# Causal attention on TensorE: scores by blocks of 32 queries instead of 64, values in four rounds, tokens in natural order

## The chip, the core and the metric

The kernel runs on one core of a Trainium2 chip, as one program. The time is device microseconds of one execution; each version is executed several times and the median counts. The engines have their own instruction streams: TensorE (PE in the profile; PEld is its weight load), VectorE (DVE), ScalarE (ACT), GpSimd (POOL) and SyncE (SP), on whose queue nearly all DMAs are issued one after another. TensorE multiplies from SBUF into the accumulation memory PSUM; a matmul has a weight tile, which is loaded first, and streams columns past it. Every value here is fp32, and an fp32 matmul leaves two matmul records in the trace.

## The reference

The input x has 64 sequences of 128 tokens and 512 features. There are 16 heads of width 64 that all share one key and one value per token, and one null key and value ahead of the first token.

```python
xn = layernorm(x, g_in)
q = (xn @ Wq).reshape(b, n, H, DH).transpose(0, 2, 1, 3) * scale      # 64 x 16 x 128 x 64
k, v = xn @ Wkv split in two                                           # 64 x 128 x 64 each
k, v = null key and value (from cond) put ahead of the tokens          # 129 keys
sim = einsum('bhid,bjd->bhij', q, k) + bias                            # bias 16 x 128 x 129
sim = where(causal_mask or masked key, -max, sim)
attn = softmax(sim)
out = einsum('bhij,bjd->bhid', attn, v).reshape(b, n, 1024) @ Wo
return x + layernorm(out, g_out)
```

The causal mask lets query i see the null key and the tokens 0 to i. Beside it every sequence has its own mask of valid keys.

## The kernel before, in words

**Stages.** The order of all work on all engines is written out by hand: a function such as `turn` calls helpers, each of which issues the instructions of one step, and each engine takes its instructions in that order. The sequences go in groups of four (GB) and in 32 pairs (PAIRS). One period of the steady state is `turn(d)` and `body(d)`. `turn(d)` (L1024 to L1050) runs the scores of the two sequences a = 2d and b = 2d + 1 and the values of the pair before. `body(d)` (from L1311) runs the projections: queries of the next group by Strassen-like products, keys and values (`kv_pair`, L363), the layernorm of the tokens, and the products with Wo of the pair before. Below a sequence is called a batch, as in the code. The first and last pairs have orders of their own: a start that is written out (L1559 to L1678) and `turn_end`, `body_end` and `body_last`.

**Scores.** The queries of two heads lie above each other on the partitions: rows 0 to 63 one head (r = 0), rows 64 to 127 the other (r = 1). The key tile kT holds the keys twice, on both halves; the upper copy is made by a DMA (L396). A score matmul (L718) uses a 64 by 64 quarter of the array: 64 rows of features and 64 columns of weights, which are 64 queries of one head. So four matmuls, for (r, u) in 2 x 2, run at a time. The queries of a sequence are cut into two halves (hf): half 0, the tokens 0 to 63, gets the first 64 keys (NL); half 1 gets all 128. For each half there are four such groups (f) and four matmuls in each. On the partitions of the result lie 64 queries of head group u = 0 and 64 of u = 1; on the free axis eight heads (R8). A row of S is ROW = 1 + 64 + 128 + 1 = 194 elements: the null key and the keys of half 0, the keys of half 1 and the null key again.

**Softmax.** `bias_add` (L683, GpSimd) fills S with bias plus mask. `scores_add` (L733, L735, VectorE) adds the scores from PSUM. `scores_max` (L740) takes the maximum, `exps` (L749, ScalarE) exponentiates a row (queries on the partitions) of one head and half, with its sum, `rinv` (L767) inverts the sums, `scale` (L771, GpSimd) multiplies. `mask_neg` (L670, ScalarE) turns the byte mask of a group, loaded by `load_mask` (L137), into large negative numbers.

**Values.** `blocks_T` (L787, VectorE) transposes S in blocks of 32 by 32 into the tile sb, so that 32 keys of one block lie on each quarter of the partitions. A values matmul (L849) has 32 rows (the keys of block j) by 64 columns (the values, vr); quarter s of the rows holds the queries of block s. Eight places, (s, r) in 4 x 2, run at a time. In each place four matmuls follow one another, the first with 256 columns and three with 128. `WIDE` merges two of the 128s into one 256 for s = 3 in some turns. The order of tokens within a sequence is changed so that these rounds come out: `PLACE = 0, 1, 3, 2` swaps the third and the fourth block of 32 tokens. For this the copies out of PSUM that write the transposed tokens xT (`norm_T`, L313 and L315) and the keys kT (`kv_pair_out`, L380 to L396) are made in three pieces. `values_out` (L868, L870, ScalarE) copies the result with the null value added to oT.

**The start.** `load_bias` (L193 to L203) loads the bias of the heads in the layout of S with six DMAs for each u (L198 and L200), called from `load_second` (L177). It stands on SP's queue ahead of the key copies (L396) that `kv_pair_out` issues, of `load_mask(0)` and of the copies of the values by way of DRAM (`values_T`, vd L406 and vr L411). `causal` (L212, GpSimd) writes the causal mask into the bias, three instructions for each u; `null_shift` (L225, L229, VectorE) subtracts the null key's bias. On ScalarE `mask_neg(0)` stands ahead of the copies of qT for `q_batches((6,))` (L459) and of `norm_T(6)`; the first scores, `scores(0, 0)`, come on TensorE behind `norm_T(7)`. The very first matmuls of the program are `keep_busy` (L1556), products of the identity that nobody reads.

Of the kernel before, what the change touches and what calls it, by code (L numbers as in the profile page):

```python
# [17 lines left out]
def kernel(  # L18
# [63 lines left out]
    P = 128  # L82
# [11 lines left out]
    NL = DH  # L94
    ROW = 1 + NL + N + 1
    LK, UK = slice(1, 1 + NL), slice(1 + NL, 1 + NL + N)
    assert NQ == GB and NQ == KC
    PLACE = 0, 1, 3, 2
# [48 lines left out]
    nbp = const.tile([P, R8], FP, name="nbp")  # L147
    nv2 = const.tile([P, 1], FP, name="nv2")
    nbh = const.tile([P, H], FP, name="nbh")
    biasp = const.tile([P, R8, ROW], FP, name="biasp")  # L150
# [42 lines left out]
    def load_bias(u):  # L193
        rows = slice(u * DH, (u + 1) * DH)
        bias_r = attn_bias.rearrange("(u f r) i j -> u r i f j", u=2, r=2)[u]
        for r in range(2):
            rf = slice(r * NF, (r + 1) * NF)
            nc.sync.dma_start(out=biasp[rows, rf, LK], in_=bias_r[r, 0:DH, :, 0:NL])  # L198
            for i, at in enumerate((N - Q, N - 2 * Q)):
                nc.sync.dma_start(  # L200
                    out=biasp[u * DH + i * Q : u * DH + (i + 1) * Q, rf, UK],
                    in_=bias_r[r, at : at + Q],
                )  # L203

    def causal(u):

        for rows, keys, base in (
            (slice(u * DH, (u + 1) * DH), LK, 0),
            (slice(u * DH, u * DH + Q), UK, N - Q),
            (slice(u * DH + Q, (u + 1) * DH), UK, N - 2 * Q),  # L210
        ):
            nc.gpsimd.affine_select(  # L212
                biasp[rows, :, keys],
                biasp[rows, :, keys],
                pattern=[[0, R8], [-1, keys.stop - keys.start]],
                compare_op=ALU.is_ge,
                fill=NEG,
                base=base,
                channel_multiplier=1,
            )  # L220

    def null_shift(u):

        rows = slice(u * DH, (u + 1) * DH)
        nc.vector.tensor_copy(  # L225
            nbp[rows].rearrange("p (r f) -> p r f", r=2),
            nbh[rows, u * R8 : (u + 1) * R8].rearrange("p (f r) -> p r f", r=2),
        )
        nc.vector.tensor_tensor(  # L229
            biasp[rows, :, 1 : ROW - 1],  # L230
            biasp[rows, :, 1 : ROW - 1],
            nbp[rows].unsqueeze(2).broadcast_to([DH, R8, NL + N]),
            ALU.subtract,
        )
# [11 lines left out]
    nc.gpsimd.memset(biasp[0:DH], 0.0)  # L246
    nc.gpsimd.memset(biasp[DH:, :, 0 : ROW : ROW - 1], 0.0)
# [7 lines left out]
    nc.gpsimd.memset(mneg[:, :, 0 : ROW : ROW - 1], 0.0)  # L255

# [49 lines left out]
    def norm_T(m):  # L306
        g, t = divmod(m, GB)
        if t == 0:
            xT[g] = gp.tile([P, GB, KC, N], FP, tag="xT", name=f"xT_{g}")
        xh = xs.pop(m)  # L310
        pt = ps_w.tile([P, KC, P], FP, tag="w", name=f"pxT_{m}")
        for kc in range(KC):
            nc.tensor.transpose(pt[:, kc, :], xh[:, kc * P : (kc + 1) * P], ident)  # L313
        for at, to, n in ((0, 0, 2), (3, 2, 1), (2, 3, 1)):
            nc.scalar.copy(  # L315
                xT[g][:, t, :, to * Q : (to + n) * Q], pt[:, :, at * Q : (at + n) * Q]
            )
# [3 lines left out]
    def tokens_T(m):  # L321

        g, t = divmod(m, GB)
        if t == 0:
            xbs[g] = hp.tile([P, NQ, KC, NQ, Q], FP, tag="xb", name=f"xb_{g}", bufs=1)
        nc.vector.transpose(
            xbs[g][:, :, :, PLACE[t], :].rearrange("p j c q -> p c j q"),
# [22 lines left out]
    kT = hp.tile([P, NQ, GB, Q], FP, tag="kT", name="kT", bufs=1)  # L350
# [24 lines left out]
    def kv_pair_out(m, pkv):  # L375
# [11 lines left out]
        src = pkv[K_ROWS].rearrange("p (t i q) -> p t i q", t=2, i=NQ)  # L387
        out = kT[K_ROWS, :, two].rearrange("p i t q -> p t i q")
        for at, to, n in ((0, 0, 2), (3, 2, 1), (2, 3, 1)):
            nc.scalar.activation(  # L390
                out[:, :, to : to + n],
                src[:, :, at : at + n],
                AF.Identity,
                bias=nkv[K_ROWS],
            )
        nc.sync.dma_start(out=kT[V_ROWS, :, two], in_=kT[K_ROWS, :, two])  # L396
# [31 lines left out]
    def q_tiles(g, fs, tags):  # L428
        units = [(f, h) for f in fs for h in range(2)]
        for (f, h), tag in zip(units, tags):  # L430
            qT[g, f, h] = gp.tile(
                [P, GB // 2, 2, 2, DH], FP, tag=tag, name=f"qT_{g}_{f}_{h}", bufs=1
# [25 lines left out]
    def q_copy(pq, c, h):  # L458
        nc.scalar.copy(  # L459
            q_part(0, c, h), pq.rearrange("p t (h i) -> p t h i", h=2)  # L460
        )
# [67 lines left out]
    def q_out(g, c, h, tag, name=None):  # L529
        o = q_part(g, c, h)  # L530
        p = prod[tag].rearrange("p (t h i) -> p t h i", t=2, h=2)
        if name is None:
            nc.scalar.copy(o, p)
        else:
            k = kept.pop(name).rearrange("p (t h i) -> p t h i", t=2, h=2)
# [54 lines left out]
    def inner_out(g, h, f, t, at, name=None):  # L590

        o = q_part(g, 2 * h + f, 0)[:, t]
        p = inner[g, h][:, at].rearrange("p (h i) -> p h i", h=2)
        k = o
        if name is not None:
            k = kept[name].rearrange("p (t h i) -> p t h i", t=2, h=2)[:, t]
# [59 lines left out]
    def last_out(g, h, f, t, at, first=False):  # L656

        o = q_part(g, HC + 2 * h + f, 0)[:, t]
        p = last_area(g, h, at).rearrange("p (h i) -> p h i", h=2)
        k = o  # L660
        if first:
            k = base[f].rearrange("p (t h i) -> p t h i", t=2, h=2)[:, t]
# [4 lines left out]
    def mask_neg(g):  # L667
        m8 = m8s.pop(g).rearrange("p (t j) -> p t j", t=GB)
        for keys, m in ((LK, m8[:, :, 0:NL]), (UK, m8)):
            nc.scalar.activation(  # L670
                mneg[:, :, keys], m, AF.Identity, bias=neg, scale=-NEG
# [4 lines left out]
    def bias_add(b, parts=(slice(0, ROW),)):  # L676
        g, t = divmod(b, GB)
        if b < B - 1:
            S[b] = sp.tile([P, R8, ROW], FP, tag="s", name=f"s_{b}", bufs=3)
        else:  # L680
            S[b] = hp.tile([P, R8, ROW], FP, tag="xb", name=f"s_{b}", bufs=1)
        for keys in parts:
# [5 lines left out]
                .broadcast_to([P, R8, keys.stop - keys.start]),  # L688
# [3 lines left out]
    KEYS = LK, UK  # L692
    WITH_NULL = slice(0, 1 + NL), slice(1 + NL, ROW)

    def rooms(b, hf, tiles):

        nk = N if hf == 1 else NL
        return [
            pool.tile([P, NF, nk], FP, tag=tag, name=f"sc_{b}_{hf}_{tag}")
# [3 lines left out]
    def scores(b, hf, tiles=None):  # L703
        g, t = divmod(b, GB)
        nk = N if hf == 1 else NL
        if tiles is None:
            whole = ps_s.tile([P, 2, NF * nk], FP, tag="s", name=f"ps_{b}_{hf}")
            whole = whole.rearrange("p r (f j) -> p r f j", f=NF)
# [5 lines left out]
        for f in range(NF):  # L714
            for r in range(2):
                rows = slice(r * DH, (r + 1) * DH)
                for u in range(2):
                    nc.tensor.matmul(  # L718
                        home[r][u * DH : (u + 1) * DH, f, :],
                        qT[g, f, t // 2][rows, t % 2, hf, u],  # L720
                        kT[rows, 0 : nk // Q, t, :],
                        start=True,
                        stop=True,
                    )
# [12 lines left out]
    def scores_max(b, hf):  # L737
        if hf == 0:
            nmax[b] = small.tile([P, 2, R8], FP, tag="nmax", name=f"nmax_{b}")
        nc.vector.tensor_reduce(  # L740
            nmax[b][:, hf], S[b][:, :, WITH_NULL[hf]], AX.X, ALU.max, negate=True
        )

    def exps(b, hf, lo=0, hi=R8):
        if hf == 0 and lo == 0:
            rsum[b] = small.tile([P, 2, R8], FP, tag="rsum", name=f"rsum_{b}")
        for k in range(lo, hi):
            row = S[b][:, k, WITH_NULL[hf]]
# [20 lines left out]
    def scale(b, hf, lo=0, hi=R8):  # L769
        sv = S[b][:, lo:hi, KEYS[hf]]  # L770
        nc.gpsimd.tensor_tensor(  # L771
            sv,
            sv,
            rinvs[b, hf][:, lo:hi].unsqueeze(2).broadcast_to([P, hi - lo, sv.shape[2]]),
            ALU.mult,
        )
# [6 lines left out]
    def blocks_T(b, lo=0, hi=R8):  # L783

        if lo == 0:
            sbs[b] = hp.tile([P, 6, R8, Q], FP, tag="sb", name=f"sb_{b}")
        nc.vector.transpose(  # L787
# [936 lines left out]
```

## Time and profile before

| | us |
|---|---|
| median of three runs | 1023.52 |
| lowest and highest of them | 1023.01, 1023.75 |
| span of the profiled execution | 1021.2 |
| TensorE busy in it | 1012.8 (99%) |
| VectorE busy | 845.8 (83%) |
| GpSimd busy | 769.2 (75%) |
| ScalarE busy | 673.1 (66%) |

The span runs from the first to the last instruction that the profile shows; the runs' times hold a little more around it, 2.3 us by the median. A row of the groups has line, engine, operation, tiles and shapes, the count, then the busy time, the mean of one in ns and the idle time ahead of it. The chain and the timeline have start and length in us, engine, what, and how many records stand in a row; "[1.35 <-POOL neg L245]" means idle before, and what ended it. Overlapping records of TensorE make a group's mean longer than what one adds to the time: four or eight small matmuls run side by side.

### The profile page before, as it was taken

To read this page: it belongs to the slowest core of one execution; us is meant where nothing else is said; L and a number is where in the kernel's file an instruction comes from. 1 tells how busy PE (TensorE), PEld (TensorE's weight loads), DVE (VectorE), ACT (ScalarE), POOL (GpSimd) and SP (SyncE) were. 2 spreads that over 40 slices of the span, in tenths; PEclk is the share of its full clock that TensorE was granted. 3 is DMA by queue.
4 is the path that set the end of the run, shared out by engine and by line. 5 is a ranking of instruction groups with operands and counts; after the bars stand their busy time and mean duration, and the time that the engine had idled before them with its cause. 6 is when DMAs were issued, how large, how long until landed. Compare 5 with 4: busy or idle time off the path is not lost.

```text
span 1021.2 us, 31459 instructions
## 1 busy us (share of the span) xinstructions
PE 1012.8 (99%) x12333; PEld 899.6 (88%) x12333; DVE 845.8 (83%) x1958; ACT 673.1 (66%) x2753; POOL 769.2 (75%) x633
## 2 busy tenths in 40 slices
PE   9999999999999999999999999999999999999997
PEld 8888888888888888888888888888888888888886
DVE  6777888888888888888888888888898888977787
ACT  5766677656677665686656776566775657865583
POOL 4997768677686877859678696776868768686686
PEclk9999999999999999999999999999999999999999
DMA  7415143151531415225152341514315152140221
GB/s 219 139 30 151 67 122 112 36 154 63 144 98 69 123 56 152 88 74 140 36 152 85 109 120 32 164 63 138 102 50 134 64 152 89 71 111 24 69 85 62
DMA packets 73835, 100.86 MB, mean 99 GB/s; under 512 B 32212, under 2 KB 36056, under 8 KB 71896
## 3 DMA queue, kind: packets, MB, share of 16 engines
q1 hardware_dynamic: 73392, 98.47, 32.5%
q8 instruction: 96, 1.57, 0.6%
q14 instruction: 51, 0.42, 0.1%
q10 hardware_dynamic: 296, 0.40, 0.1%
HBM read 63.19 MB, written 33.55 MB: 95 GB/s over the span
## 4 chain that ended last, share of the span: by engine, by line
PE 96%; POOL 1%; DVE 1%; ACT 1%; issue 0%; DMA 0%; POOLq 0%; DVEq 0%; ACTq 0%
PE pyX L936 20%; PE pa L515 16%; PE pyY L936 10%; PE pc L515 10%; PE po L849 8%; PE pkv L363 6%; PE pyw L936 5%; PE pl L581 4%; PE pm L647 4%; PE ps L718 3%; PE pq L450 3%; PE sc_X L718 2%; PE sc_Y L718 2%; PE sc_a L718 1%; PE py_s L936 1%; ACT s L749 1%
## 5 line engine op out<-in xcount | busy, mean ns | idle before, releaser
L749 ACT ACTIVATE s<-s,nmax 128x65 f32<-128x65 f32 (+1 forms) x1024 | 372.2, 369 | 61.7 <-DVE nmax L740 61.7
L771 POOL TENSOR_TENSOR s<-s,rinv 128x512 f32<-128x512 f32 (+1 forms) x132 | 190.6, 1446 | 133.1 <-DVE rinv L767 133.1
L683 POOL TENSOR_TENSOR s<-biasp,mneg 128x1552 f32<-128x1552 f32 (+1 forms) x65 | 206.2, 3176 | 50.9 <-DVE s L733 26.9
L749 ACT ACTIVATION_READ_ACCUMULATOR s<-s,nmax 128x1 f32 x1024 | 197.1, 192 | 0.0
L787 DVE STREAM_TRANSPOSE sb<-s 128x1536 f32<-128x1536 f32 (+1 forms) x68 | 113.6, 1674 | 11.4 <-POOL s L771 11.4
L740 DVE TENSOR_REDUCE nmax<-s 128x8 f32<-128x1032 f32 (+1 forms) x128 | 121.8, 952 | 0.1
L964 ACT COPY y<-pyX 128x256 f32<-128x256 f32 x29 | 10.8, 372 | 167.5 <-PE pyX L936 129.7
L936 PE MATMUL pyX<-wT,oT 128*128 128x256 f32 x464 | 109.7, 379 | 0.0
L936 PE MATMUL pyX<-wo,oT 128*128 128x256 f32 x464 | 109.7, 379 | 0.0
L936 PEld LDWEIGHTS pyX<-wo,oT 128*128 128x128 f32 x464 | 86.0, 190 | 10.5
L936 PEld LDWEIGHTS pyX<-wT,oT 128*128 128x128 f32 x464 | 84.0, 190 | 9.2
L916 POOL TENSOR_TENSOR oT<-oT 128x512 f32<-128x512 f32 x64 | 80.6, 1277 | 3.9 <-PE pyw L936 1.6
L849 PE MATMUL po<-sb,vr 32*64 32x128 f32 (+1 forms) x3904 | 82.9, 308 | 0.2 <-DVE sb L787 0.2
L527 ACT COPY ku<-pa 128x256 f32<-128x256 f32 x118 | 43.4, 367 | 59.8 <-issue 30.8
L849 PEld LDWEIGHTS po<-sb,vr 32*64 32x64 f32 x3904 | 71.7, 130 | 9.4 <-issue 5.6
L536 DVE TENSOR_TENSOR qT<-pc,ku 128x256 f32<-128x256 f32 x118 | 48.2, 408 | 32.2 <-PE pc L515 19.7
L868 ACT ACTIVATE oT<-po,nv 128x512 f32<-128x512 f32 (+1 forms) x127 | 73.5, 655 | 0.4 <-PE po L849 0.2
L515 PE MATMUL pa<-xS,wq 128*128 128x256 f32 x264 | 67.8, 379 | 0.0
L597 DVE TENSOR_TENSOR qT<-pl,kp 128x128 f32<-128x128 f32 x112 | 32.1, 286 | 42.8 <-PE pl L581 41.9
L281 POOL TENSOR_TENSOR rstd<-rstd,nhalf 128x1 f32<-128x1 f32 x64 | 35.2, 557 | 42.0 <-DVE rstd L280 38.9
L363 PE MATMUL pkv<-xT,wkv 128*128 128x256 f32 x256 | 63.3, 391 | 0.0
L515 PE MATMUL pa<-xT,wq 128*128 128x256 f32 x236 | 60.6, 379 | 0.0
(207 smaller groups left out, 2588.9 us busy)
## 6 DMA issues: line engine op xcount, KB each, us to landing
res<-in_x_dram SPq DMA_DIRECT2D x64, 256.0 KB
out_dram<-y SPq DMA_DIRECT2D x63, 256.0 KB
x<-in_x_dram SPq DMA_DIRECT2D x62, 256.0 KB
xd<-xb SPq DMA_DIRECT2D x14, 1024.0 KB
xT<-xd SPq DMA_DIRECT2D x56, 256.0 KB
vr<-vd SPq DMA_DIRECT2D x64, 128.0 KB
kT<-kT SPq DMA_DIRECT2D x32, 64.0 KB
vd<-vb SPq DMA_DIRECT2D x32, 64.0 KB
```

The lines of the kernel that those rows point to most:

```text
L363: nc.tensor.matmul(pkv, wkv[:, kc, :], xT[g][:, t : t + 2, kc, :], start=(kc == 0), stop=(kc == KC - 1),)
L515: nc.tensor.matmul(prod[tag], w[:, kc, f * P : (f + 1) * P], t[:, :, kc, :], start=(start and kc == 0), stop=(kc == HK - 1), skip_group_ch ...
L683: nc.gpsimd.tensor_tensor(S[b][:, :, keys], biasp[:, :, keys], mneg[:, t, keys] .unsqueeze(1) .broadcast_to([P, R8, keys.stop - keys.start ...
L718: nc.tensor.matmul(home[r][u * DH : (u + 1) * DH, f, :], qT[g, f, t // 2][rows, t % 2, hf, u], kT[rows, 0 : nk // Q, t, :], start=True, st ...
L740: nc.vector.tensor_reduce(nmax[b][:, hf], S[b][:, :, WITH_NULL[hf]], AX.X, ALU.max, negate=True)
L749: nc.scalar.activation(row, row, AF.Exp, bias=nmax[b][:, hf, k : k + 1], accum_out=rsum[b][:, hf, k : k + 1],)
L771: nc.gpsimd.tensor_tensor(sv, sv, rinvs[b, hf][:, lo:hi].unsqueeze(2).broadcast_to([P, hi - lo, sv.shape[2]]), ALU.mult,)
L787: nc.vector.transpose(sbs[b][:, :, lo:hi].rearrange("p j e q -> p e j q"), S[b][:, lo:hi, 1 : ROW - 1].rearrange("p e (j k) -> p e j k", k=Q),
L849: nc.tensor.matmul(po[s][rows, to : to + n], vr[g][quad, t, PLACE[j], :], sb[quad, slots, r * NF : (r + 1) * NF, :], start=(turn == 0), st ...
L868: nc.scalar.activation(to, src, AF.Identity, bias=nv2)
L916: eng.tensor_tensor(o, a, b, op)
L936: nc.tensor.matmul(prod[key], h[:, c, :], w[:, c, :], start=(start and c == 0), stop=(c == HC - 1), skip_group_check=not start,)
```

## The change

Queries are taken in blocks of 32 (i = 0 to 3) instead of 64, and block i gets its own (i + 1) x 32 keys. A weight tile of a score matmul is still 64 columns wide: 32 queries of two heads. A batch has, as before, 64 score matmuls: for each i four groups of four, with 32, 64, 96 and 128 columns where half of them had 64 and half 128. On the partitions of S lie four quarters of 32 queries, each with heads of its own; the free axis has four heads (NE) and ROW = 324 elements, with the keys of the four blocks and a null key at both ends of each half.

- `load_bias`: 16 DMAs for each u instead of six, each for 32 partitions and two heads. `causal`: eight instructions for each u instead of three. `null_shift`: four instead of two.
- `mask_neg`: four instructions for each group instead of two. `scores_max` and `scale`: two for each half, one for each block, instead of one. `exps`: 16 for each batch as before, of 33, 65, 97 and 129 elements instead of 65 and 129. `blocks_T`: three pieces for each batch instead of one.
- `values`: four rounds j = 0 to 3. In round j all eight places run block j of the keys for all later queries, with 256, 192, 128 and 64 columns. `WIDE` is gone. The four quarters are now head groups and not query blocks. `values_out` copies in the order 0, 2, 1, 3.
- Tokens keep their natural order: `PLACE` is gone, and `norm_T` and `kv_pair_out` copy in one piece instead of three.
- At the ends, `turn_end`, `body_end` and `body_last` take over the new pieces; the order of the steps is otherwise as it was, in `turn` and in the start too.

```diff
-    NL = DH
-    ROW = 1 + NL + N + 1
-    PLACE = 0, 1, 3, 2
+    NE = H // NQ
+    NF2 = NF // 2
+    KEYS_OF = tuple((i + 1) * Q for i in range(NQ))
+    ROW = NQ + sum(KEYS_OF)
+    LOW = 2 + sum(KEYS_OF[:2])
+    K_AT = 1, 1 + Q, LOW + 1, LOW + 1 + KEYS_OF[2]
+    BLOCK = tuple(slice(K_AT[i], K_AT[i] + KEYS_OF[i]) for i in range(NQ))
+    KEYS = slice(1, LOW - 1), slice(LOW + 1, ROW - 1)
...
     def load_bias(u):
+        bias_r = attn_bias.rearrange("(v u f r) i j -> u v r i f j", v=2, u=2, r=2)[u]
+        for i in (3, 2, 1, 0):
+            for v in range(2):
+                quad = slice((2 * u + v) * Q, (2 * u + v + 1) * Q)
+                for r in range(2):
+                    nc.sync.dma_start(
+                        out=biasp[quad, r * NF2 : (r + 1) * NF2, BLOCK[i]],
+                        in_=bias_r[v, r, i * Q : (i + 1) * Q, :, 0 : KEYS_OF[i]],
+                    )
...
-        for at, to, n in ((0, 0, 2), (3, 2, 1), (2, 3, 1)):
-            nc.scalar.copy(
-                xT[g][:, t, :, to * Q : (to + n) * Q], pt[:, :, at * Q : (at + n) * Q]
-            )
+        nc.scalar.copy(xT[g][:, t], pt)
...
-        for f in range(NF):
-            for r in range(2):
-                rows = slice(r * DH, (r + 1) * DH)
-                for u in range(2):
-                    nc.tensor.matmul(
-                        home[r][u * DH : (u + 1) * DH, f, :],
-                        qT[g, f, t // 2][rows, t % 2, hf, u],
-                        kT[rows, 0 : nk // Q, t, :],
-                        start=True,
-                        stop=True,
-                    )
+        for i in BLOCKS[hf]:
+            keys = slice(BLOCK[i].start - first, BLOCK[i].stop - first)
+            for f in range(NF2):
+                for r in range(2):
+                    rows = slice(r * DH, (r + 1) * DH)
+                    for u in range(2):
+                        nc.tensor.matmul(
+                            home[r][u * DH : (u + 1) * DH, f, keys],
+                            qT[g, u * NF2 + f, t // 2][rows, t % 2, i],
+                            kT[rows, t, 0 : KEYS_OF[i]],
+                            start=True,
+                            stop=True,
+                        )
...
-    def values(b, wide=()):
+    def values(b):
...
+        for j in range(NQ):
+            slots = slice(j * (1 + SLOT), j + SLOT * SLOT + 1, SLOT)
             for s in range(NQ):
                 quad = slice(s * Q, (s + 1) * Q)
                 for r in range(2):
                     nc.tensor.matmul(
-                        po[s][rows, to : to + n],
-                        vr[g][quad, t, PLACE[j], :],
-                        sb[quad, slots, r * NF : (r + 1) * NF, :],
-                        start=(turn == 0),
+                        pos[b][s][r * DH : (r + 1) * DH, :, j * Q :].rearrange(
+                            "p f (i q) -> p f i q", q=Q
+                        ),
+                        vr[g][quad, t, j, :],
+                        sb[quad, slots, r * NF2 : (r + 1) * NF2, :].rearrange(
+                            "p i f q -> p f i q"
+                        ),
+                        start=(j == 0),
                         stop=True,
...
-        values(p, WIDE if 4 < d < PAIRS - 1 else ())
-        values(p + 1, WIDE if 4 < d < PAIRS - 1 and (d % 2 or d % 10 == 4) else ())
+        values(p)
+        values(p + 1)
```

More of the change, by code (lines that the diff above doesn't have):

```diff
@@ L216, in causal @@
[L216 to L219, printed above, removed]
-            )
[L222 to L227, printed above, removed]
-        )
[L229 to L234, printed above, removed]
+                nbp[rows].unsqueeze(2).broadcast_to([DH, NE, keys.stop - keys.start]),
@@ L386, in kv_pair_out @@
         )
[L387 to L396, printed above, removed]
+        nc.scalar.activation(
+            kT[K_ROWS, two],
+            pkv[K_ROWS].rearrange("p (t n) -> p t n", t=2),
+            AF.Identity,
+            bias=nkv[K_ROWS],
+        )
+        nc.sync.dma_start(out=kT[V_ROWS, two], in_=kT[K_ROWS, two])
     def values_T(g):
@@ L668, in mask_neg @@
         m8 = m8s.pop(g).rearrange("p (t j) -> p t j", t=GB)
-        for keys, m in ((LK, m8[:, :, 0:NL]), (UK, m8)):
+        for keys, n in zip(BLOCK, KEYS_OF):
             nc.scalar.activation(
-                mneg[:, :, keys], m, AF.Identity, bias=neg, scale=-NEG
+                mneg[:, :, keys], m8[:, :, 0:n], AF.Identity, bias=neg, scale=-NEG
             )
```

224 lines of the change are left out of this document (119 added, 105 removed).

## The prediction

> **What bounds the kernel now.** I read the busy times and the chain of waits on the page first, then the chain in order of time for two turns in the middle.
>
> ```profile
> PE 1012.8 (99%) x12333; PEld 899.6 (88%) x12333; DVE 845.8 (83%) x1958; ACT 673.1 (66%) x2753; POOL 769.2 (75%) x633
> ...
> PE 96%; POOL 1%; DVE 1%; ACT 1%; issue 0%; DMA 0%; POOLq 0%; DVEq 0%; ACTq 0%
> ```
>
> TensorE is busy for 99% of the span and 96% of the chain is its matmuls. So a microsecond is won only where TensorE has less to do, and lost where it is made to wait. In the chain below the columns are start, length, what, and the number of records; every fp32 matmul leaves two records.
>
> ```profile
> 511.09 0.67 PE pl L581 x6
> ...
> 527.80 0.20 PE sc_Y L718 x2
> ...
> 528.02 0.04 PE sc_Y L718 x2
> ...
> 528.84 0.04 PE sc_a L718 x2
> ...
> 528.90 0.88 PE ps L718 x32
> ...
> 530.65 2.56 PE po L849 x116
> 533.21 1.92 PE pkv L363 x8
> 535.13 0.86 PE pa L515 x4
> ...
> 558.98 0.20 PE sc_Y L718 x2
> ...
> 561.82 2.46 PE po L849 x103
> 564.29 1.93 PE pkv L363 x8
> ...
> 590.06 0.20 PE sc_Y L718 x2
> ```
>
> Turns start at 527.80, 558.98 and 590.06, 31.1 us apart, with no gap. Scores take 2.85 us of a turn (527.80 to 530.65), values 2.5 (530.65 to 533.21; 561.82 to 564.29). Only these 5.3 us change; the other 25.8 us keep their matmuls.
>
> **Scores on TensorE.** A 256-column record takes 0.86/4 = 0.215 us, 0.84 ns a column. In scores four records run side by side, one in each quarter of the array. With 128 columns a group of four takes 0.88/8 = 0.110 us (0.108 by columns). With 64 columns it takes (528.84 - 528.02)/14 = 0.0586, where the columns alone would take 0.054. Weights explain the difference: 128-column records under 128-column weights take 0.67/6 = 0.112, longer than under 64-column weights, so the load paces there, and half as many weight columns give about 0.056 to 0.058. A batch now has 8 groups of 64 and 8 of 128 columns: 8 x 0.0586 + 8 x 0.110 = 1.35 us. After the change it has 4 groups each of 32, 64, 96 and 128 columns, all with 64-column weights. The 96s take about 0.083. The 32s are bounded by 0.027 (columns) and 0.0586 (no gain); I take 0.0586, because the load stays. That is 4 x (0.0586 + 0.0586 + 0.083 + 0.110) = 1.24, -0.107 a batch, -0.21 a turn; with the other bound -0.47.
>
> [...]
>
> **Values on TensorE.** Eight records run side by side. Both versions push 640 columns through each of the eight places per batch; the rounds of 256, 128, 128, 128 become 256, 192, 128, 64. By columns alone nothing changes, and the last records get 64 columns shorter (-0.05 a turn). But the records don't flow freely:
>
> ```profile
> core 0: us, PE busy (x) PEld busy (x), PEclk, DMA share, GB/s
> 561.74:562.36 0.62, 0.61 (x27) 0.54 (x33) 1.00 0.00 0
> 562.36:562.42 0.06, 0.06 (x22) 0.06 (x9) 1.00 0.00 0
> ```
>
> These stretches show L849 alone. 33 weight loads start in the first 0.62 us, then none in the next 0.06: the nine there are still running. So 33 loads wait ready when values begin, and the 34th comes some 0.03 us after the second record of the first place has ended (start 0.27 + length 0.37). From there a place's two records follow every 0.0167 us. Stepping the 128 records through these three rules puts the last start at 2.25, 2.27 and 2.28 us after the first for none, both or one of the two batches with the merged matmuls (WIDE), as the trace has it. For the new order it gives 2.40: the smaller the rounds, the more records are unfinished at a time, and the short rounds run into the limit. The next matmul follows 0.20 us after a 128-column start and 0.15 after a 64-column one. Mean of the 29 regular turns before 2.48, after 2.55: +0.065 a turn. Bounds: -0.1 (columns, shorter end) and +0.3 (the short rounds at the densest pace of 128-column records, 13.6 ns a record); I take the stepped value, since the same rules give the three cases that the trace has.
>
> Turns: 29 x (-0.213 + 0.065) = -4.3 us.
>
> **Other engines in a turn.** They get lighter, and have room.
>
> ```profile
> L749 ACT ACTIVATE s<-s,nmax 128x129 f32<-128x129 f32 x512 | 200.0, 397 | 0.0
> L749 ACT ACTIVATE s<-s,nmax 128x65 f32<-128x65 f32 x512 | 172.2, 341 | 61.7 <-DVE nmax L740 61.7
> L735 DVE TENSOR_TENSOR s<-ps,s 128x1024 f32<-128x1024 f32 x33 | 40.2, 1217 | 0.7 <-POOL s L683 0.7
> L787 DVE STREAM_TRANSPOSE sb<-s 128x1536 f32<-128x1536 f32 x60 | 106.2, 1770 | 11.4 <-POOL s L771 11.4
> L787 DVE STREAM_TRANSPOSE sb<-s 128x768 f32<-128x768 f32 x8 | 7.4, 956 | 0.0
> L683 POOL TENSOR_TENSOR s<-biasp,mneg 128x1552 f32<-128x1552 f32 x63 | 202.9, 3222 | 49.0 <-DVE s L733 26.9 <-DVE sb L787 13.2 <-DMA vd<-vb 8.9
> L771 POOL TENSOR_TENSOR s<-s,rinv 128x1024 f32<-128x1024 f32 x60 | 115.2, 1920 | 115.7 <-DVE rinv L767 115.7
> L771 POOL TENSOR_TENSOR s<-s,rinv 128x512 f32<-128x512 f32 x72 | 75.4, 1051 | 17.4 <-DVE rinv L767 17.4
> ```
>
> Per batch: an exponential costs 0.9 ns an element and a fixed part, so sixteen rows of 33, 65, 97 and 129 save 0.22 us on ScalarE. Sums and bias go from 1536 and 1552 elements to 1280 and 1296: -0.25 us on VectorE, -0.5 on GpSimd. The transpose is 0.14 + 1.06 ns an element: three for 1280 cost 1.78, as now. Maxima likewise: twice the instructions, fewer elements, no difference. Scaling is 0.18 + 1.70 ns: four of 128 to 512 elements cost 2.9, now 2.97. None lands on TensorE; nor do the four mask instructions instead of two, which run before the first maximum while ScalarE waits 1.3 us. If that cover went, values would be copied out late and the first output product would wait. Outside the 29 turns: four scores pairs at either end and shorter last softmax work, -0.9 in all. An occasional turn whose instructions come late (the 2.56 above against 2.46) I count three times more: +0.3.
>
> **The start.** Here the change adds DMAs: 32 bias loads instead of 12, all on SP's queue, ahead of the key copies, the first mask and the value copies.
>
> ```profile
> 14.25 2.49 SPq L200 DMA_DIRECT2D biasp<-in_fside_16xSxS_dram  x2
> 16.93 0.35 SPq L184 DMA_DIRECT2D nbh<-cond_null_attn_bias_dram  x1
> 17.32 0.60 SPq L198 DMA_DIRECT2D biasp<-in_fside_16xSxS_dram  x1
> ...
> 20.90 1.45 SPq L396 DMA_DIRECT2D kT<-kT  x2
> 22.41 0.59 SPq L137 DMA_DIRECT2D m<-in_mask_BxS_bk_dram  x1
> 23.09 1.30 SPq L406 DMA_DIRECT2D vd<-vb  x2
> 26.33 1.73 SPq L411 DMA_DIRECT2D vr<-vd  x4
> ...
> 26.25 1.15 ACT L670 ACTIVATE mneg<-m,neg 128x256 f32<-128x256 uint8 x2
> 27.27 0.38 ACT L459 COPY qT<-pq 128x256 f32<-128x256 f32 x1
> 27.52 0.74 ACT L315 COPY xT<-pxT 128x256 f32<-128x256 f32 x3
> ...
> 1.35 3.35 PE L1556 MATMUL busy<-wR 128*128 128x128 f32 x14 [1.35 <-POOL neg L245]
> ...
> 4.80 1.38 PE L1556 MATMUL busy<-wR 128*128 128x128 f32 x10
> ...
> 29.41 0.27 PE L718 MATMUL sc_Y<-kT,qT 64*64 64x64 f32 x2
> ```
>
> Until about 16 us the early loads hold the queue back in both versions, and six bias loads get out. Then 26 DMAs remain where 7 remained. The four vr issues took 0.43 each and 0.465 with the gap; the bias ones ran at 0.60 (17.32 to 20.90, six). Bounds for the new, smaller ones: 0.35 (nbh) and 0.60. I take 0.47, the nearest row by size (32 partitions). The key copies then start at about 28 instead of 20.9, the mask at 29.2 instead of 22.41. A landing takes about 2.6 us (vd's second issue at 23.8, vr freed by it at 26.33): the mask is there at 31.8, where it had been in time before 26.25. ScalarE works in order: behind the mask it has the copy of qT and the copy of xT out of the PSUM buffer that the first scores need. Four mask instructions cost 2.0, the two copies 0.85: 34.6. TensorE stood ready at 29.41: +5.2 us, with +2.9 and +8.5 at the bounds. The masked bias on GpSimd (ready at about 36) comes after these scores and holds nobody.
>
> Standing for 5 us has a second price. The first 14 matmuls of the program took 3.35 us, 0.24 each, later ones 0.11. If TensorE starts slowly again, about 1.7 us more; if not, 0. I take 1.7, since the only start from rest in the trace is slow. [...]
>
> **Sum.** On the profiled execution: 1021.2 - 4.3 - 0.9 + 0.3 + 5.2 + 1.7 = 1023.2 us of span. The median of the runs is 2.3 us above that span, so 1025.5 us.
>
> **Rivals.** (1) Faster: the small bias DMAs issue at 0.35 each, the wait is 2.9 us and the clock stays up: 1021.2 - 4.9 + 2.9 + 2.3 = 1021.5; with the 32-column groups at 0.027 another 7.4 us less, which the 0.112 row speaks against. Chance 0.24, the larger half for the 32-column groups, which no row shows: they alone would give 1018.1. (2) No change: the wait is as forecast but TensorE doesn't start slowly: 1023.8. Chance 0.26. (3) Slower than forecast: the bias DMAs keep 0.60: wait 8.5, slow start, 1028.8. Chance 0.13. (4) The short value rounds don't get denser than 13.6 ns a record: +0.3 instead of +0.065 a turn, +6.8: 1032; for it speaks that no row is denser, against it that a short round is only 16 records, which can wait ready. Chance 0.08. [...] (5) The change doesn't do what it says, for the start's mask could be waited for elsewhere; nothing in the order of ScalarE allows it.
>
> **How the numbers follow.** The forecast with a slow start has 0.29. From no change 0.2% (2.0 us) can be told. Forecast, (3) and (4) are slower: 0.50. (2) gives the same: 0.26; (1) faster: 0.24. The range 1019.5 to 1030.5 leaves out the deep half of (1) and all of (4), 0.2 together. The forecast's own range, for its two bounds, is 1023 to 1028.
>
> **What would show it.** Right: scores about 2.63 us a turn, values about 2.55 to the next matmul, turns of 30.93 us, 32-column groups no faster than 64-column ones; bias issues until 28 us; an idle TensorE of some 5 us near 29 us ended by ScalarE's copy of xT, and slow matmuls after it. Wrong: no such idle time, 32-column groups near 0.03, or turns that wait for VectorE or ScalarE.

## The result and the profile after

The changed kernel takes 1034.82 us (median of four runs, 1032.21 to 1035.52) against 1023.54: the ratio is 1.0108, with a 95% interval of 1.0094 to 1.0122. It is slower by 11.3 us, where 2.0 were forecast; the measured time lies above the range.

The page of the changed kernel, its busy times, its instruction loads and its chain:

```profile
span 1033.2 us, 32182 instructions
PE 1016.9 (98%) x12493; PEld 903.5 (87%) x12493; DVE 809.8 (78%) x2216; ACT 666.1 (64%) x2705; POOL 736.1 (71%) x768
...
q8 instruction: 98, 1.61, 0.6%
...
PE 95%; DMA 2%; SPq 1%; POOL 1%; issue 1%; ACT 0%; POOLq 0%; DVE 0%; DVEq 0%
```

TensorE is still the bound, VectorE, ScalarE and GpSimd have become lighter as forecast, and 2% of the chain is DMA and 1% SP's queue, which had no share before. The row q8 will matter: 98 loads of instructions, 1.61 MB.

Two turns in the chain of the changed kernel (start, length, what, records):

```profile
538.15 0.18 PE sc_Y L731 x2
538.33 0.01 PE sc_w L731 x2
...
538.78 0.02 PE sc_a L731 x2
...
540.78 2.73 PE po L869 x102
543.51 1.92 PE pkv L367 x8
...
569.28 0.18 PE sc_Y L731 x2
...
571.91 1.30 PE po L869 x57
573.21 0.06 issue
573.27 1.46 PE po L869 x56
574.72 1.92 PE pkv L367 x8
```

Scores now take 2.63 us (538.15 to 540.78; 569.28 to 571.91), exactly what was forecast. But values take 2.73 us in the first turn and 2.81 in the second, and in the middle of the second the chain says "issue": TensorE waited for nothing that the profile shows. The start of the changed kernel, on SP's queue, ScalarE and TensorE:

```profile
9.18 11.91 SPq L203 DMA_DIRECT2D biasp<-in_fside_16xSxS_dram  x16
...
21.61 7.48 SPq L203 DMA_DIRECT2D biasp<-in_fside_16xSxS_dram  x16
29.19 1.17 SPq L397 DMA_DIRECT2D kT<-kT  x2
30.41 0.58 SPq L141 DMA_DIRECT2D m<-in_mask_BxS_bk_dram  x1
...
33.52 1.92 ACT L671 ACTIVATE mneg<-m,neg 128x128 f32<-128x128 uint8 x4 [7.25 <-DMA m<-in_mask_BxS_bk_dram]
...
35.75 0.42 PE L731 MATMUL sc_Y<-kT,qT 64*64 64x32 f32 x2 [6.01 <-ACT qT L460]
```

The bias loads fill the queue until 29.1 us, the mask comes 7.25 us late to ScalarE, and TensorE stands for 6.0 us. What follows it, in stretches of TensorE (length, busy time, PEclk as the granted clock):

```profile
core 0: us, PE busy (x), PEclk, DMA share, GB/s
29.44:35.75 6.31, 0.30 (x4) 0.83 0.34 76
35.75:40.40 4.65, 4.59 (x66) 0.50 0.42 111
40.40:43.23 2.83, 2.83 (x14) 1.00 0.51 137
```

For 4.65 us TensorE works at half its clock, which costs 2.3 us more. Before, it worked through 25 to 34 us at 1.00:

```profile
25.00:34.00 9.00, 9.00 (x111) 1.00 0.42 104
```

Where the 12.0 us of span (1033.2 - 1021.2) went, by the first score record of turns 1 and 29 in both traces:

| | forecast | measured |
|---|---|---|
| start, until turn 1 (60.48, now 69.03) | +6.9 | +8.55 |
| 28 turns (871.4, now 875.0) | -4.0 | +3.5 |
| after the start of turn 29 (89.3, now 89.2) | -0.9 | -0.1 |

Of the turns, the shorter scores and longer values are in: a turn in which nothing is late takes 30.95 us against 31.08 before, -3.6 in 28. The other +7.1 is lateness: a turn is called late here when its values take longer than in the turns on time. In 9 of 29 turns the last record of values starts 2.41 or 2.42 us after the first, in 20 later, by up to 0.73 us. (One of the 9, turn 7, loses 0.5 us right behind its last values record instead.) Before, 3 turns of 29 were late, by 0.1 to 0.2.

A late turn and one on time in the changed kernel, L869 alone, cut at the same places after the first values record (0.68 and 1.16 us):

```profile
core 0: us, PE busy (x) PEld busy (x), PEclk, DMA share, GB/s
696.67:697.35 0.68, 0.67 (x27) 0.58 (x30) 1.00 0.00 0
697.35:697.83 0.48, 0.34 (x17) 0.00 (x0) 1.00 0.00 0
697.83:699.60 1.77, 1.76 (x97) 1.77 (x98) 1.00 0.03 9
```

```profile
759.60:760.28 0.68, 0.67 (x29) 0.60 (x34) 1.00 0.00 0
760.28:760.76 0.48, 0.48 (x48) 0.48 (x33) 1.00 0.13 34
760.76:762.01 1.25, 1.25 (x87) 1.25 (x77) 1.00 0.00 0
```

In the late turn 30 weight loads start and then none for 0.48 us, while 17 matmuls that are in flight end; then the other 98 run on. The profile names no operand that they wait for, and the same matmuls run on in the turn on time. That points to the instructions themselves.

**The theory.** TensorE has 12493 pairs of weight load and matmul, 24,986 instructions, and 98 loads of instructions come in the queue q8: 255 for each load, and 257 before (24,666 / 96). I take a load as 256 instructions or 128 pairs. (A load is 16.4 KB, 1.61 MB / 98, some 64 bytes an instruction.) Scores and values are 256 pairs in 5 us, two loads' worth. The theory is that TensorE waits where it reaches the end of one load, the seam, before the next is usable. A turn of the changed kernel has 388 pairs and a few other instructions, so the seam moves through the dense stretch by some 7 pairs a turn (4 of them are the pairs above 3 x 128). Before, the merged matmuls (WIDE) left 380 or 384 pairs and it nearly stood still. The rivals are that the short rounds themselves cost, and that other DMAs disturb at random.

### The profile page after: what moved, and what is told of

It reads as the page before. It is cut to its first block, busy times and chain, and to the rows that moved or that the text cites. A ratio compares the mean times of both kernels' runs of the same rounds, so it can differ in the third digit from the quotient of the medians.

```text
span 1033.2 us, 32182 instructions
## 1 busy us (share of the span) xinstructions
PE 1016.9 (98%) x12493; PEld 903.5 (87%) x12493; DVE 809.8 (78%) x2216; ACT 666.1 (64%) x2705; POOL 736.1 (71%) x768
## 3 DMA queue, kind: packets, MB, share of 16 engines
q8 instruction: 98, 1.61, 0.6%
## 4 chain that ended last, share of the span: by engine, by line
PE 95%; DMA 2%; SPq 1%; POOL 1%; issue 1%; ACT 0%; POOLq 0%; DVE 0%; DVEq 0%
PE pyX L953 19%; PE pa L516 15%; PE pyY L953 10%; PE pc L516 10%; PE po L869 8%; PE pkv L367 6%; PE pyw L953 5%; PE pl L582 4%; PE pm L648 4%; PE ps L731 3%; PE sc_X L731 2%; PE sc_Y L731 2%; PE pq L451 1%; PE py_s L953 1%; PE sc_a L731 1%; SPq L203 1%
## 5 line engine op out<-in xcount | busy, mean ns | idle before, releaser
L767 ACT ACTIVATE s<-s,nmax 128x33 f32<-128x33 f32 (+3 forms) x1024 | 357.9, 354 | 30.5 <-DVE nmax L754 30.5
L791 POOL TENSOR_TENSOR s<-s,rinv 128x128 f32<-128x128 f32 (+3 forms) x256 | 181.7, 732 | 117.8 <-DVE rinv L785 117.7
L684 POOL TENSOR_TENSOR s<-biasp,mneg 128x1296 f32<-128x1296 f32 (+1 forms) x65 | 188.3, 2899 | 85.9 <-ACT mneg L671 58.5
L754 DVE TENSOR_REDUCE nmax<-s 128x4 f32<-128x132 f32 (+3 forms) x256 | 112.5, 482 | 0.1
L821 DVE STREAM_TRANSPOSE sb<-s 128x256 f32<-128x256 f32 (+3 forms) x194 | 103.9, 587 | 0.6 <-POOL s L791 0.5
L869 PE MATMUL po<-sb,vr 32*64 32x256 f32 (+1 forms) x4064 | 90.3, 304 | 2.1 <-issue 2.0
L869 PEld LDWEIGHTS po<-sb,vr 32*64 32x64 f32 x4064 | 79.5, 130 | 14.1 <-issue 11.5
```

Source lines behind the costliest of these rows:

```text
L684: nc.gpsimd.tensor_tensor(S[b][:, :, keys], biasp[:, :, keys], mneg[:, t, keys] .unsqueeze(1) .broadcast_to([P, NE, keys.stop - keys.start ...
L754: nc.vector.tensor_reduce(nmax[b][:, hf, k * NE : (k + 1) * NE], S[b][:, :, WITH_NULL[i]], AX.X, ALU.max, negate=True,)
L767: nc.scalar.activation(row, row, AF.Exp, bias=nmax[b][:, hf, k : k + 1], accum_out=rsum[b][:, hf, k : k + 1],)
L791: nc.gpsimd.tensor_tensor(sv, sv, rinvs[b, hf][:, k : k + NE] .unsqueeze(2) .broadcast_to([P, NE, KEYS_OF[i]]), ALU.mult,)
L821: nc.vector.transpose(sbs[b][:, at : at + n].rearrange("p j e q -> p e j q"), S[b][:, :, keys].rearrange("p e (j k) -> p e j k", k=Q),)
L869: nc.tensor.matmul(pos[b][s][r * DH : (r + 1) * DH, :, j * Q :].rearrange("p f (i q) -> p f i q", q=Q), vr[g][quad, t, j, :], sb[quad, slo ...
```

## The experiments

### The merged matmuls taken out of the kernel before

```diff
-        values(p, WIDE if 4 < d < PAIRS - 1 else ())
-        values(p + 1, WIDE if 4 < d < PAIRS - 1 and (d % 2 or d % 10 == 4) else ())
+        values(p)
+        values(p + 1)
```

> The kernel before, with its merged values matmuls (WIDE) taken out, so that each turn has 128 pairs of weight load and matmul in values and 388 in all, as after the change; rounds of 256, 128, 128, 128 columns, scores, layout and start as before. Theory A (instruction supply): TensorE's instructions come in loads of 16 KB, which is 256 instructions or 128 pairs; with 388 pairs and a few other instructions a turn the seam between two loads wanders through the 256 dense pairs of scores and values, and where it lies badly TensorE waits for the next load. Then this kernel gets the late turns too: values spread from 2.25 to about 3.1 us, more than half of the turns late, 4 to 9 us in all: 1027 to 1033 us. Theory B (the short rounds of the new order are what costs): none of them is here, values stay at 2.25 us: 1023.0 to 1023.5 us.

Measured: 1030.98 us, ratio 1.0078 (1.0059 to 1.0096), with 20 late turns of 29 (by more than 0.03 us). The instruction loads of the kernel before, and then of this one:

```profile
q8 instruction: 96, 1.57, 0.6%
```

```profile
q8 instruction: 98, 1.61, 0.7%
```

Turn 16 in this kernel, L849 alone:

```profile
533.76:535.18 1.42, 1.42 (x72) 1.25 (x72) 1.00 0.26 98
535.18:535.48 0.30, 0.30 (x9) 0.01 (x1) 1.00 0.27 102
535.48:536.25 0.77, 0.77 (x43) 0.74 (x44) 1.00 0.25 96
```

Turn 15 in the changed kernel, L869 alone:

```profile
509.13:510.65 1.52, 1.51 (x71) 1.36 (x72) 1.00 0.00 0
510.65:511.02 0.37, 0.37 (x8) 0.00 (x0) 1.00 0.00 0
511.02:512.16 1.14, 1.14 (x56) 1.11 (x56) 1.00 0.07 14
```

Both kernels lose their loads behind the 72nd pair of values, one turn apart, though rounds, layout and times differ. What the two places share is the count: of all TensorE records in the trace in order of start (weight loads, matmuls, semaphore instructions and a few others), the stop comes behind number 12,993 in this kernel and behind number 12,225 in the changed one, exactly 3 x 256 apart. The place is given by the count of instructions. The old rounds show the lateness, so the new ones are not its cause. And the merge, worth nothing by the columns, is what kept the kernel before on time.

### The seam made to stand still, at two places

Three or four of the 64 values matmuls are left out from turn 5 on; then, in a second kernel, seven more in turn 4 alone.

```diff
+                    if (j, s, r) in out:
+                        continue
...
-        values(p)
-        values(p + 1)
+        some = d > 4
+        values(p, ((3, 0, 0), (3, 0, 1)) if some else ())
+        values(p + 1, ((3, 0, 0), (3, 0, 1))[: 1 + (d % 3 == 0)] if some else ())
```

> The changed kernel, but from turn 5 on three (in each third turn four) of the 64 values matmuls are left out: those of the last round (64 columns) for the tile s = 0, so the last 32 queries of four heads miss their last key block. A turn then has 381 or 382 pairs instead of 388, as before the change, and with the other instructions about 3 x 128: the seam no longer wanders. Theory A: it stays where turn 5 has it (16 pairs into scores and values, no late values there), late turns go away from turn 5 on, 6 to 8 us less: 1027 to 1029 us, where the matmuls left out have themselves no more than 0.1 us a turn. Rival (late turns come by chance, from traffic of the other DMAs): 1032 to 1035 us.

> As after_fewer_values, and in turn 4 alone seven more of the last-round values matmuls are left out, so that all later turns begin 14 pairs earlier in the stream of instructions: the seam stands still again, but some 30 instead of 16 pairs into scores and values. There the changed kernel had turns 0.25 to 0.6 us late (its turns 21 and 22). Theory A: nearly all 25 turns are late by about that much, 6 to 15 us more than after_fewer_values (1027.9): 1034 to 1043 us, with seven matmuls fewer. Rival (fewer matmuls help by themselves, wherever the seam is): 1027 to 1028 us.

Measured: 1027.89 us (ratio to the kernel before 1.0041, 1.0028 to 1.0055) and 1037.54 us (1.0142, 1.0128 to 1.0155). In the first, 24 of the 25 turns from turn 5 on have values at 2.365 us and a length of 30.91; in the second 22 of 25 are late, by 0.43 us in the mean over the 25. All that separates them in these turns is 14 pairs of position; a disturbance at random would not tell the two apart. Two turns of the second kernel in its chain:

```profile
544.20 0.92 PE po L871 x26
545.12 0.34 issue
545.46 1.97 PE po L871 x75
547.43 1.92 PE pkv L367 x8
...
575.83 0.92 PE po L871 x24
576.75 0.09 issue
576.83 2.09 PE po L871 x77
```

The stop comes behind the 26th record of values in one turn and the 24th in the next; in all turns from turn 5 on with a stop of over 0.2 us it lies between the 22nd and the 28th. The 16 and 30 of the table below are the places as planned; by the stops the second seam stands at 22 to 28, and the first, 14 pairs less, at 8 to 14. Values, first to last record start (us), in some turns of the runs so far and of the one with 16 bias loads below:

```
turn                     5     8    12    15    19    22    24    26
before                2.27  2.28  2.28  2.27  2.27  2.28  2.27  2.28
before, not merged    2.25  2.99  2.49  2.74  2.61  2.30  2.25  2.25
after                 2.41  3.14  2.54  3.03  2.97  2.91  2.41  3.13
after, 16 bias loads  2.41  2.86  2.85  3.19  3.25  2.88  2.41  3.56
seam standing at 16   2.37  2.37  2.37  2.37  2.37  2.37  2.37  2.37
seam standing at 30   2.89  2.79  2.54  2.94  2.72  3.12  3.10  2.84
```

The packets of q8 give the time that is needed. Values in the thirteen kernels told of here, the one before among them, have 60 stops of more than 0.3 us behind the first 16 records. 58 of them end 1.25 to 1.60 us after the end of the last instruction load, 2.2 to 2.9 us after its start. This holds whether the stop lies at the 24th or the 124th record. And the same 58, in eleven kernels with different rounds, starts and orders, all come behind a TensorE record whose number, counted as above, is a multiple of 256 plus 193: the stop stands at one place of each 256 instructions and nowhere else. (The other two, among the last pairs of the kernel before and of the unmerged one, end 12.5 and 3.5 us after a load, are not at that place, and have another cause.) The scatter between the runs is then that of when a load ends; whether its start or its length, 0.9 to 2.2 us, makes it was not taken apart.

### The same instructions with the dense stretch cut in two

```diff
-        po = values_rooms(p)
...
+            pkvs[d] = kv_pair(g * GB + 2 * (d % 2), (ps_y, "Y"))
+            po = values_rooms_s(p)
...
         values(p)
         values(p + 1)
...
+                pkv = pkvs.pop(d)
...
-            pkv = kv_pair(g * GB + 2 * h)
```

> The changed kernel, with the key and value products of the next group (8 records, 1.92 us) moved from behind values to between scores and values (in the PSUM room Y; the third values tile takes the room s instead). Same number of instructions, same matmuls. Theory A: the two dense stretches of 128 pairs are 1.9 us apart, so two seams are never less than some 4 us apart, and a load that takes some 3.9 us from the crossing of one seam to its use comes in time: nearly all late turns go, 6 to 8.5 us less, 1026 to 1029 us. Theory B: rounds and columns are the same, 1034 to 1036 us; a new wait for a PSUM room would show as a gap at the first values matmul and make it slower.

Measured: 1064.58 us, ratio 1.0404 (1.0388 to 1.0419). On the lateness it says what theory A said: in all 29 turns values take 2.405 to 2.407 us. (The 3.9 us in it was an estimate of mine that no run shows.) But every turn has become longer by 1.25 us or more (32.20 and 32.26), by a wait that I had not counted. The waits of TensorE and its weight loads in this kernel (total, times, longest):

```profile
PE pa L516 <- ACT oT L907: 20.8, 29, 0.8
```

```profile
PEld pa L516 <- ACT oT L907: 24.8, 29, 0.9
PEld pl L582 <- ACT oT L907: 12.0, 28, 0.4
```

The key and value product behind values had covered ScalarE's copies out of the PSUM rooms (buffers) of values. With it gone, the first products of the body wait for their rooms.

### The bias in 16 loads

```diff
-        bias_r = attn_bias.rearrange("(v u f r) i j -> u v r i f j", v=2, u=2, r=2)[u]
+        bias_r = attn_bias.rearrange("(v u e) i j -> u v i e j", v=2, u=2)[u]
...
-                for r in range(2):
-                    nc.sync.dma_start(
-                        out=biasp[quad, r * NF2 : (r + 1) * NF2, BLOCK[i]],
-                        in_=bias_r[v, r, i * Q : (i + 1) * Q, :, 0 : KEYS_OF[i]],
-                    )
+                nc.sync.dma_start(
+                    out=biasp[quad, :, BLOCK[i]],
+                    in_=bias_r[v, i * Q : (i + 1) * Q, :, 0 : KEYS_OF[i]],
+                )
...
```

> The changed kernel with the four heads of a partition in natural order, so that the bias of both r comes with one DMA: 16 instead of 32 bias loads, same bytes and same pieces. Theory A for the start: the number of DMA issues on SP's queue sets when the key copies and the mask go out. The mask is issued at about 24 us instead of 30.4, ScalarE's mask step is no longer late, TensorE has no gap of 6.0 us and no half clock after it (2.3 us): 8.3 us less, 1026.5 us. Rival: bytes or descriptors set it, not issues: no change, 1035 us. The turns behind the start keep their late values in either case, since no instruction of TensorE changes.

Measured: 1027.72 us, ratio 1.0047 (1.003 to 1.0064), 7.1 us less than the changed kernel. SP's queue, ScalarE and the clock in this kernel:

```profile
9.37 8.11 SPq L202 DMA_DIRECT2D biasp<-in_fside_16xSxS_dram  x8
...
18.00 3.76 SPq L202 DMA_DIRECT2D biasp<-in_fside_16xSxS_dram  x8
21.85 1.18 SPq L396 DMA_DIRECT2D kT<-kT  x2
23.08 0.58 SPq L141 DMA_DIRECT2D m<-in_mask_BxS_bk_dram  x1
```

```profile
26.21 1.92 ACT L670 ACTIVATE mneg<-m,neg 128x128 f32<-128x128 uint8 x4
```

```profile
29.00:34.00 5.00, 5.00 (x83) 1.00 0.37 96
```

Half as many issues with the same bytes, each still 0.47 us (3.76 / 8), and the mask is there in time; there is no stop and no half clock, and turn 1 begins at 60.18 us (69.03 in the changed kernel, 60.48 before). The start is won back in full, 8.85 us in the profiles; the turns are 1.2 us later in this profile than in that of the changed kernel (876.2 against 875.0 for the 28), as the scatter of late turns has it.

### Both edits

> Both of the two edits before. Theory A: the two gains are at different places and add up, 14 to 17 us less than the changed kernel: 1018 to 1021 us, faster than the kernel before (steady turns of 30.95 us against 31.09). If only one of the theories on turns and start holds, 1026 to 1029 us; if neither, 1035 us.

Measured: 1055.52 us, ratio 1.0318 (1.0303 to 1.0333), 9.1 less than with the cut alone. Late turns (none) and start (turn 1 at 60.5) are as expected; the uncounted wait is there again, with turns of 32.20 and 32.26 us.

### Only a part of the product between scores and values

On top of the 16 bias loads, the values tiles move to other rooms, and one, none or two of the four steps of the contraction stay behind values. The first of the three:

```diff
+            pkvs[d] = kv_pair(g * GB + 2 * h, (ps_y, "Y"), range(3))
...
         values(p)
         values(p + 1)
...
+            kv_part(g * GB + 2 * h, pkvs[d], range(3, KC))
```

> The changed kernel with 16 bias loads, and three of the four contraction steps of the key and value product (6 records, 1.44 us) between scores and values, the fourth behind values. The values tiles of s = 1 and 3 lie in the PSUM room s, those of s = 0 and 2 in the two rooms w, the key and value product in Y, so that the first product behind values (room a) waits for no copy. Theory A: late turns need the seams nearer than some 3.9 us; 2.4 + 1.44 is just about that, so values stay at 2.41 us in nearly all turns; the copies of s = 0 and 2 end some 1.45 us behind values, under the 0.48 + 0.86 + 0.22 us of work that TensorE has there: no new wait. Turns of 30.95 us: 1018.5 to 1019.5 us. If the gain of the earlier run came from something else than the distance of the seams, or the copies are needed earlier, 1024 us and more.

> As split_3_1, with all four steps (1.92 us) between scores and values. Theory A: no late turn at all, values at 2.41 us; behind values TensorE has only 0.86 + 0.22 us before the first output product, which needs the copies of s = 0 and 2 (1.45 us): a wait of some 0.4 us a turn, 11 us in all: 1029 to 1031 us.

> As split_3_1, with two steps (0.96 us) between and two behind values. Theory A: the seams are 2.4 + 0.96 = 3.4 us apart in the bad positions, some 0.5 us less than a load takes: turns that were 0.5 to 0.75 us late are late by 0 to 0.3, about 2 us in all; perhaps 0.1 us a turn of waiting for the room s. 1020 to 1024 us, between split_3_1 and the changed kernel with 16 bias loads (1027.7).

Measured: 1034.22 us (ratio 1.0104, 1.009 to 1.0118), 1045.39 (1.0216, 1.0202 to 1.023) and 1025.1 (1.0017, 1.0008 to 1.0026). Values are on time in all turns of the first two and in 25 of 29 of the third, where 0.96 us lie between. The turns are another matter: 31.43 and 31.55 us, 31.85 and 31.98, and 31.15. The first two expectations missed a wait, and the third run lies 1 us above its range. Weight loads that wait in the kernel with three steps between:

```profile
PEld pa L519 <- ACT ku L531: 5.8, 14, 0.4
PEld pa L519 <- POOL rstd L287: 5.3, 10, 0.5
```

The copies of values come nearer to the products behind them, and ScalarE's copies out of room a, which stand behind those in its order, are later for the next product there. (The row that names GpSimd I read as the same wait; that was not tried.) With two steps behind values these waits are absent, and 0.20 us remain of the 31.15. I read them as the price of one more change from large tiles to small and back: the first values record now starts 0.31 us after the last large one, where it started 0.20 after a score record, and in the chain the two halves of the product take 1.06 us each, where the whole took 1.92. The best of these is faster than the one with 16 bias loads, and still slower than the kernel before.

### Together

> After_fewer_values with the 16 bias loads. Theory: the two causes are independent and add up to the whole loss: 7 us at the start and 7 us in the turns, 1020 to 1021.5 us, below the kernel before (with three or four value matmuls a turn left out, as in after_fewer_values).

Measured: 1018.15 us, ratio 0.9952 (0.9937 to 0.9967): with the seam standing still at a good place and the start mended, the changed scores and values are 0.5% faster than the kernel before, less what the three or four matmuls save (values at 2.365 instead of 2.405 us, 1.0 us over 25 turns). It is 2 us less than expected: turn 1 begins 8.1 us earlier than without the 16 bias loads (60.83, 68.97), where 7 were counted; the rest was not followed up. That kernel leaves out a part of the work, though. A complete one, with the cut only where the seam lay worst:

> Complete kernel, 16 bias loads, with half of the key and value product between scores and values (as split_2_2) only in the 13 turns whose seam lay worst in the two profiles so far (2, 7, 8, 12, 15, 16, 17, 19, 20, 21, 22, 26, 27). Theory A: the seams lie where they did, since no instruction is added or taken; the 13 turns lose 0.48 us of lateness each and pay 0.2 us for one more change between large and small tiles, 3.6 us in all, against 1027.7: 1023.5 to 1024.5 us, about the kernel before.

Measured: 1023.74 us, ratio 1.0005 (0.9997 to 1.0014), the same as before, as expected. Its profile shows that the choice of turns rested on a wrong premise, so that the time came out is in part luck: turns 3, 4, 9 and 10, at most 0.29 us late in the two profiles from which I chose, are 0.33 to 0.78 us late here. The seam had not moved: ahead of these turns TensorE has one record less than in the kernel with 16 bias loads. So at one and the same place the lateness differs from run to run. No complete kernel tried is faster than the one before.

## Why the prediction was wrong

**The step that failed** is the last sentence on the other engines: "An occasional turn whose instructions come late ... I count three times more: +0.3." It came to +7.1. I took lateness for chance, and multiplied what I saw. The runs show it as a function of position: the kernel before had few late turns because its merged matmuls held the seam still, and the change took them out. I costed them by columns, in the values step, where they only cost 0.02 us a turn. The material was there: the profile's page counts 96 instruction loads against 12333 pairs, and the three late turns (2, 4 and 16) all have 124 or 128 pairs in values.

**The start** had the right mechanism, place and order, and was too small: 5.2 + 1.7 forecast, 6.0 + 2.3 measured, of 8.55 in all. Six bias loads were out by 16 us, as assumed, and from 17.4 us on an issue took 0.47 (7.48 / 16). Two things were missed: the two issues in between took 1.3 us, and the load of nbh, between the two halves of the bias, was not among the 26. So the mask was issued at 30.41 instead of 29.2, and it was there 3.1 us later (33.52), not 2.6. The wait ended with ScalarE's copies as forecast, but already with that of qT; that of xT held the next records by some 0.2 us more. The slow stretch is the granted clock: 0.50 for 4.65 us, until 40.40, behind 6.0 us of rest; how long a rest brings it no run shows.

**Right:** scores at 2.63 us a turn and 32-column groups no faster than 64-column ones. In the chain, eight groups of four records take 538.78 - 538.33 = 0.45 us, 0.056 each; the first four have 32 columns. (Groups are counted in records here, as are the 64 score matmuls of a batch ahead of the prediction.) The bound of 0.0586 decided, and not that by columns (0.027); that the weight loads set it was my estimate. The trace has 14 ns for a record of 32 columns (0.056 for four). Values that are not late start their last record at 2.405 us (stepped: 2.40), and the next matmul follows 0.147 later (0.15); so rival (4) plays no part. A turn that is not late takes 30.95 us (30.93). The other engines stayed out of the way.

**The ends** gave -0.1 instead of -0.9. Turn 29 and the last values pairs are late too, by 0.35 us and up to 1; I did not take them apart further.

**The rivals.** (1) and (2) needed a shorter wait or no slow clock, and had neither. (3), 1028.8, let each bias load after 16 us take 0.60, and they took 0.47 from 17.4 us on; its wait of 8.5 us was 6.0. None named the position in the instruction stream, which decided, and so the range ended 4 us short.

**What stays open:** when the load is asked for isn't in any record, so the 3.7 to 3.9 us from crossing one seam to using the next load, which I used for the cuts, are an estimate that no run shows. In the changed kernel the 11 stops of more than 0.3 us in values end 3.1 to 3.5 us after TensorE passed the place 256 records earlier, counted as above. The distance of two seams alone does not decide: with the seam standing at the earlier place TensorE goes from one seam to the next in 2.6 to 2.8 us without a stop, and with it 14 pairs on it stops. Why values are seldom late while the seam lies in their first 14 pairs is not shown. Why three of 25 turns with the seam at 30 were on time, and one of 25 with the seam at 16 late, was not followed up.

## What to carry to other kernels

Where a kernel has dense stretches of small matmuls, count the instructions of a period as well as their columns: here a load of 256, with the stop ending 1.25 to 1.6 us after its last packet, set the time. Its position relative to the stretch was worth 10 us between two kernels that differ in seven matmuls. An "issue" gap without a missing operand was the sign of it (0.06 to 0.34 us in the chains above), and a merge worth 0.02 us a turn by columns held the position. Before work is moved off the place behind a stretch, look at which copies it covers.

## What was not expected of the hardware

- In these kernels TensorE's instructions came in loads of 255 to 257 by the counts (98 and 96 loads); in dense stretches of small matmuls it stopped in some turns at one place of each 256, until 1.25 to 1.60 us after the end of a load (58 stops, of 0.3 to 1.07 us).
- Half of the key and value product between scores and values, two stretches of small matmuls, cost 0.20 us a turn beyond the matmuls themselves (31.15 us against 30.95).
- The first eight bias issues took some 8.1 us with loads of 24 and 32 KB and of 16 to 64 KB alike, in the changed kernel with the DMA engines busy for 87% of that time; from then on each took 0.47 us, on the same queue.
